# Issuing most of each x load from GpSimd as half rows in a pairwise bilinear kernel

## The chip, the cores and the metric

The kernel runs on one core of a Trainium2 chip. The metric is device time in microseconds (us), as the median of several executions; before the change it is 1336.65 us (1336.59 to 1337.08 over three). The profile is one execution with the hardware profiler, with a span of 1335.1 us.

## The reference

For 4096 samples with F = 32 features of D = 64 numbers each, every pair of features i < j (496 pairs) has its own 64 x 64 matrix. The output holds, for every sample and pair, the product of feature i with the pair's matrix, multiplied elementwise by feature j:

```python
i_idx, j_idx = np.triu_indices(F, k=1)
vi = inputs[:, i_idx, :]
vj = inputs[:, j_idx, :]
vdotw = jnp.einsum('bpd,pde->bpe', vi, W)
inter = vdotw * vj
return inter.reshape(B, -1)
```

All is float32. The input is 33.6 MB, the weights 8.1 MB, and the output 520 MB, so the output's bytes dominate.

## The kernel before

The samples are cut into NT = 32 tiles of 128, one sample per partition. Per tile, TensorE transposes x (in two halves), ScalarE (ACT) copies the transpose from PSUM to SBUF, TensorE multiplies it by the weights, VectorE multiplies the products in PSUM by x and writes them into a ring in SBUF, and SyncE (SP) issues four stores per tile from the ring.

x lives in a buffer of three slots, one tile each. Apart from the first and last tile, x is loaded two tiles at a time into neighbouring slots:

```python
STORES = [[0, 1], [2, 3], [4, 5, 6], [7, 8, 9, 10, 11, 12, 13, 14, 15]]
FIRST_HALF_AT, SECOND_HALF_AT = 9, 3
RING = 28160

def x_slots(NT):
    loads = [[(0, 0)]]
    for t in range(1, NT, 2):
        if t + 1 == NT:
            loads.append([(t, 1)])
        elif loads[-1][-1] == (t - 1, 2):
            loads.append([(t + 1, 0), (t, 1)])
        else:
            loads.append([(t, 1), (t + 1, 2)])
    return loads
```

This gives 17 loads: 2 of one tile and 15 of two. One load is one DMA from ACT's queue, in which each of the 128 partitions receives one contiguous row (8 KB for one tile, 16 KB for two):

```python
xbuf = const.tile([P, 3 * F * D], F32, tag="x", name="x")
...
def load_x(load):
    at = sum(len(before) for before in x_loads[: x_loads.index(load)]) * P * F * D
    n = len(load) * F * D
    s = load[0][1]
    nc.scalar.dma_start(
        out=xbuf[:, s * F * D : s * F * D + n],
        in_=x[at : at + P * n].rearrange("(p c) -> p c", p=P),
    )
```

The main loop starts the load of tile t + 1 at the start of tile t, and transposes the first half of x for tile t + 1 late in tile t (at row pair 9 of 16, within the last store's group):

```python
for t in range(NT):
    xt = slot[t]
    for load in x_loads:
        if min(load)[0] == t + 1:
            load_x(load)
    for s, group in enumerate(STORES):
        if at + store_w[s] > RING:
            at = 0
        osb = ring[:, at : at + store_w[s]]
        at += store_w[s]
        for p in group:
            if p == SECOND_HALF_AT:
                transpose_x(xt, 1)
            if p == FIRST_HALF_AT and t + 1 < NT:
                transpose_x(slot[t + 1], 0)
            ...  # matmuls into PSUM banks (line 170), VectorE multiplies into osb (lines 180, 188)
        nc.sync.dma_start(
            out=out[:, t * cols + o0 : t * cols + o0 + store_w[s]], in_=osb
        )
```

The four stores of a tile have rows of 30,208, 26,112, 31,488 and 39,168 bytes per partition, 126,976 bytes in all; the ring holds 112,640 bytes per partition. A part of the ring can be written again once the store that read it has landed.

Of the kernel before, what the change touches and what calls it, by code (L numbers as in the profile page):

```python
# [1 line left out]

# [6 lines left out]

F32 = mybir.dt.float32  # L10
ALU = mybir.AluOpType

P = 128
BANK = 512
BANKS = 8

STORES = [[0, 1], [2, 3], [4, 5, 6], [7, 8, 9, 10, 11, 12, 13, 14, 15]]

LOADS = [[0], [1], [2, 3], [4, 5, 6], [7, 8, 9, 10, 11, 12, 13, 14, 15]]
# [20 lines that stand above are left out]
@with_exitstack  # L40
def pair_bilinear_kernel(
    ctx: ExitStack,
    tc: tile.TileContext,
    x: bass.AP,
    w: bass.AP,
    out: bass.AP,
    F: int,
    D: int,
):

    nc = tc.nc
    NT = out.shape[1] * 2 // (F * (F - 1) * D)
    NPR = F // 2

    width = [(F - 1 - i) * D for i in range(F)]
    off = [sum(width[:i]) for i in range(F)]
    cols = sum(width)  # L80


    woff = [i % 2 * D + sum(width[i % 2 : i : 2]) for i in range(F)]
    store_w = [sum(width[2 * p] + width[2 * p + 1] for p in g) for g in STORES]

    const = ctx.enter_context(tc.tile_pool(name="const", bufs=1))
    psum = ctx.enter_context(tc.tile_pool(name="ps", bufs=1, space=bass.MemoryType.PSUM))

    ident = const.tile([P, P], F32, tag="ident", name="ident")
    make_identity(nc, ident)  # L90

    def runs(tl, a, b, n):

        ap = tl[:, a : a + n]
        return bass.AP(ap.tensor, ap.offset, [list(ap.ap[0]), [b - a, 2], list(ap.ap[1])])

    xbuf = const.tile([P, 3 * F * D], F32, tag="x", name="x")
    x_loads = x_slots(NT)
    slot = {t: xbuf[:, ts(s, F * D)] for load in x_loads for t, s in load}

    def load_x(load):

        at = sum(len(before) for before in x_loads[: x_loads.index(load)]) * P * F * D
        n = len(load) * F * D
        s = load[0][1]
        nc.scalar.dma_start(
            out=xbuf[:, s * F * D : s * F * D + n],
            in_=x[at : at + P * n].rearrange("(p c) -> p c", p=P),
        )

    pring = psum.tile([P, BANKS * BANK], F32, tag="pring", name="pring")
    bank = 0

    def take_banks(n):

        nonlocal bank
        if bank + n > BANKS:
            bank = 0
        got = pring[:, bank * BANK : (bank + n) * BANK]
        bank = (bank + n) % BANKS  # L120
        return got

    xT = const.tile([P, NPR * P], F32, tag="xT", name="xT")

    def transpose_x(xt, g):

        n = 2 * BANK // P
        pt = take_banks(2)
        for c in range(n):
            nc.tensor.transpose(pt[:, ts(c, P)], xt[:, ts(n * g + c, P)], ident)  # L130
        nc.scalar.copy(xT[:, ts(g, 2 * BANK)], pt)  # L131

    ring = const.tile([P, RING], F32, tag="ring", name="ring")
    at = 0

    load_x(x_loads[0])
    w_sb = const.tile([P, sum(width[0::2])], F32, tag="w", name="w")
    done = 0
    for g in LOADS:

        upto = woff[2 * g[-1]] + width[2 * g[-1]]
        nc.sync.dma_start(out=w_sb[:, done:upto], in_=w[:, done:upto])
        done = upto

    transpose_x(slot[0], 0)
# [10 lines that stand above are left out]
            o0 = off[2 * group[0]]  # L156
# [5 lines that stand above are left out]
                first = (width[2 * p] - 1) % BANK + 1  # L162
                for c1 in range(first, width[2 * p] + 1, BANK):
                    n = first if c1 == first else BANK
                    c0 = c1 - n
                    odd = width[2 * p + 1] and c1 > D
                    pm = take_banks(2)
                    for h in range(1 + bool(odd)):
                        a = woff[2 * p + h] + c0 - h * D
                        nc.tensor.matmul(  # L170
                            pm[:, h * BANK : h * BANK + n],
                            xT[h * D : (h + 1) * D, ts(p, P)],
                            w_sb[h * D : (h + 1) * D, a : a + n],
                            start=True,
                            stop=True,
                        )
                    xj = xt[:, (2 * p + 1) * D + c0 : (2 * p + 1) * D + c1]
                    o = [off[2 * p + h] - o0 + c0 - h * D for h in range(2)]
                    if odd and (c0 or c1 < width[2 * p]):
                        nc.vector.tensor_tensor(  # L180
                            runs(osb, o[0], o[1], n),
                            runs(pm, 0, BANK, n),
                            bass.AP(xj.tensor, xj.offset, [xj.ap[0], [0, 2], xj.ap[1]]),
                            ALU.mult,
                        )
                    else:
                        for h in range(1 + bool(odd)):
                            nc.vector.tensor_tensor(  # L188
                                osb[:, o[h] + h * D : o[h] + n],
                                pm[:, h * (BANK + D) : h * BANK + n],  # L190
                                xj[:, h * D :],
                                ALU.mult,
                            )
            nc.sync.dma_start(
                out=out[:, t * cols + o0 : t * cols + o0 + store_w[s]], in_=osb
            )


# [30 lines left out]
```

## Time and profile before

| what | value |
|---|---|
| median time | 1336.65 us |
| span of the profile | 1335.1 us |
| PE busy | 1160.6 us (87%) |
| VectorE (DVE) busy | 1183.4 us (89%) |
| ACT busy | 66.1 us (5%) |
| GpSimd (POOL) busy | 0.7 us |
| moved by DMA | 562.87 MB at 422 GB/s |
| VectorE waits for landed stores (line 180) | 102.6 us in 44 waits |
| from issue to landing, x loads of two tiles (median) | 20.4 us |

In the profile, a line of the page with forty digits gives the busy share in 40 equal slices of the span. "q1" is the DMA queue of SyncE and "q10" that of ACT. In the list of DMA issues the last number is the median time from issue to landing. In the chain of waits, each line has a start, a length, and what was waited for or worked on. In the timeline, the bracket at the end of a line says how long the engine was idle before it, and what ended that.

Besides these views the trace holds one record for each DMA packet, with its queue, start, duration and size. A packet here is one contiguous row, or a semaphore's write of 4 bytes at the end of a DMA on each of the 16 engines.

### The profile page before, as it was taken

What the parts mean: (1) busy time and instruction counts of PE and PEld (TensorE: products, weight loads), DVE (VectorE), ACT (ScalarE), POOL (GpSimd) and SP (SyncE); (2) the same over time, 40 slices, a digit from 0 to 9 for tenths busy, and PEclk for the clock granted to TensorE, in tenths of its full rate; (3) what the DMA queues carried; (4) which work ended last, traced back from release to release, by engine and by line L of the source; (5) the groups of instructions that cost most, each with busy time, mean ns of one, the idle gap of its engine ahead of it and who ended that gap; (6) DMA issues with size and microseconds to landing.
All of it is one profiled execution on the core that took longest, in us unless ns stands there. A gap on an engine that the chain in (4) does not pass through costs nothing.

```text
span 1335.1 us, 13080 instructions
## 1 busy us (share of the span) xinstructions
PE 1160.6 (87%) x5376; PEld 544.9 (41%) x5376; DVE 1183.4 (89%) x1376; ACT 66.1 (5%) x65; POOL 0.7 (0%) x6
## 2 busy tenths in 40 slices
PE   6998989989899898998989889798998979989893
PEld 3443334443344443444444444344443434354441
DVE  5998989989899898998989899898998989989894
ACT  0000000000000000000000000000000000000000
POOL 0000000000000000000000000000000000000000
PEclk9999999989899999998989999899999999989997
DMA  9999999999999999999999999999999999999998
GB/s 397 433 430 430 431 428 430 418 433 430 413 425 410 436 414 427 426 414 433 405 432 431 419 429 411 432 426 421 428 413 430 426 407 417 429 421 423 429 425 352
DMA packets 21659, 562.87 MB, mean 422 GB/s; under 512 B 2400, under 2 KB 2400, under 8 KB 2656
## 3 DMA queue, kind: packets, MB, share of 16 engines
q1 hardware_dynamic: 19152, 528.49, 92.8%
q10 hardware_dynamic: 2448, 33.56, 5.9%
q8 instruction: 42, 0.69, 0.2%
q14 instruction: 17, 0.14, 0.0%
HBM read 41.94 MB, written 520.09 MB: 421 GB/s over the span
## 4 chain that ended last, share of the span: by engine, by line
DMA 47%; DVE 38%; issue 9%; PE 5%; DVEq 0%; ACT 0%
DMA out_dram<-ring 46%; DVE ring L180 32%; DVE ring L188 5%; PE pring L170 5%; DMA x<-in_x_dram 1%; DVEq L180 0%; PE pring L130 0%; ACT xT L131 0%; DVEq L225 0%; DVEq L188 0%
## 5 line engine op out<-in xcount | busy, mean ns | idle before, releaser
L170 PE MATMUL pring<-w,xT 64*128 64x512 f32 (+4 forms) x4864 | 1098.4, 564 | 146.4 <-DVE ring L180 133.5
L180 DVE TENSOR_TENSOR ring<-pring,x 128x1024 f32<-128x1024 f32 (+3 forms) x1056 | 1104.1, 1108 | 131.4 <-DMA out_dram<-ring 102.6
L170 PEld LDWEIGHTS pring<-w,xT 64*128 64x128 f32 x4864 | 489.3, 191 | 711.7 <-DVE ring L180 533.0
L131 ACT COPY xT<-pring 128x1024 f32<-128x1024 f32 x64 | 64.8, 1012 | 1224.1 <-PE pring L130 1224.1
L188 DVE TENSOR_TENSOR ring<-pring,x 128x64 f32<-128x64 f32 (+3 forms) x320 | 97.7, 356 | 2.6 <-DMA out_dram<-ring 1.9
L130 PEld LDWEIGHTS pring<-ident,x 128*128 128x128 f32 x512 | 55.6, 142 | 58.8 <-DVE ring L180 50.2
L130 PE MATMUL pring<-ident,x 128*128 128x128 f32 x512 | 70.8, 282 | 8.6 <-DMA x<-in_x_dram 8.6
L131 ACT ACT_TABLE_LOAD x1 | 1.3, 1283 | 1.7 <-PEq L221 1.7
masks.py:199 POOL TENSOR_SCALAR_AFFINE_SELECT ident<-ident 128x128 f32<-128x128 f32 x1 | 0.3, 292 | 0.1
masks.py:197 POOL MEMSET ident<- 128x128 f32 x1 | 0.2, 204 | 0.3 <-POOLq L221 0.3
L221 POOL MEMSET const-bfloat16-1.0<- 128x1 bf16 x1 | 0.1, 101 | 0.0
L221 POOL MEMSET const-uint8-127<- 128x1 uint8 x1 | 0.1, 101 | 0.0
L221 POOL MEMSET const-float32-0.0<- 128x1 f32 x1 | 0.1, 98 | 0.2 <-issue 0.2
L221 POOL MEMSET const-float32-1.0<- 128x1 f32 x1 | 0.1, 98 | 0.0
## 6 DMA issues: line engine op xcount, KB each, us to landing
out_dram<-ring SPq DMA_DIRECT2D x32, 4896.0 KB, 17.7
out_dram<-ring SPq DMA_DIRECT2D x32, 3936.0 KB, 18.1
out_dram<-ring SPq DMA_DIRECT2D x32, 3776.0 KB, 18.3
out_dram<-ring SPq DMA_DIRECT2D x32, 3264.0 KB, 18.6
x<-in_x_dram ACTq DMA_DIRECT2D x15, 2048.0 KB, 20.4
w<-in_w_dram SPq DMA_DIRECT2D x1, 2592.0 KB, 28.1
x<-in_x_dram ACTq DMA_DIRECT2D x2, 1024.0 KB, 12.8
w<-in_w_dram SPq DMA_DIRECT2D x1, 2016.0 KB, 22.2
```

Source lines behind the costliest of these rows:

```text
L130: nc.tensor.transpose(pt[:, ts(c, P)], xt[:, ts(n * g + c, P)], ident)
L131: nc.scalar.copy(xT[:, ts(g, 2 * BANK)], pt)
L170: nc.tensor.matmul(pm[:, h * BANK : h * BANK + n], xT[h * D : (h + 1) * D, ts(p, P)], w_sb[h * D : (h + 1) * D, a : a + n], start=True, st ...
L180: nc.vector.tensor_tensor(runs(osb, o[0], o[1], n), runs(pm, 0, BANK, n), bass.AP(xj.tensor, xj.offset, [xj.ap[0], [0, 2], xj.ap[1]]), ALU ...
L188: nc.vector.tensor_tensor(osb[:, o[h] + h * D : o[h] + n], pm[:, h * (BANK + D) : h * BANK + n], xj[:, h * D :], ALU.mult,)
L221: nc = bacc.Bacc("TRN2", target_bir_lowering=False, num_devices=1)
```

## The change

The x load of two tiles is split by rows. Rows (partitions) 0 to 119 are issued from GpSimd, rows 120 to 127 from ACT. Each row comes as two halves of 8 KB that lie apart in DRAM, where the host has laid out all first halves of a load ahead of all second halves. The loads of one tile stay with ACT alone, and are halved as well. It is meant to take the bulk of the x loads off ACT's queue, and to let them go in smaller pieces beside the stores.

```diff
-        nc.scalar.dma_start(
-            out=xbuf[:, s * F * D : s * F * D + n],
-            in_=x[at : at + P * n].rearrange("(p c) -> p c", p=P),
-        )
+        slots = xbuf[:, s * F * D : s * F * D + n]
+        rows = x[at : at + P * n].rearrange("(h p c) -> p h c", h=2, p=P)
+        halves = slots.rearrange("p (h c) -> p h c", h=2)
+        k = P - P // 16 if len(load) == 2 else 0
+        if k:
+            nc.gpsimd.dma_start(out=halves[:k], in_=rows[:k])
+        nc.scalar.dma_start(out=halves[k:], in_=rows[k:])
...
-    x = np.concatenate([rows[:, [t for t, _ in load]].ravel() for load in x_slots(NT)])
+    x = []
+    for load in x_slots(NT):
+        of_load = rows[:, [t for t, _ in load]].reshape(P, 2, -1)
+        x.append(of_load.transpose(1, 0, 2).ravel())
+    x = np.concatenate(x)
```

## The prediction

> **What bounds the kernel now.** I read the page first, then the stretches by pair of tiles, then the chain of waits and VectorE's timeline over one pair (172 to 254 us), and last the packet records. From the page:
>
> ```profile
> DMA  9999999999999999999999999999999999999998
> ...
> q1 hardware_dynamic: 19152, 528.49, 92.8%
> q10 hardware_dynamic: 2448, 33.56, 5.9%
> ```
>
> The 16 DMA engines are full in every slice. The stores and w (q1) take 92.8% of their time, x (q10) 5.9%; instruction fetches take the rest. The stretches show the same for one pair of tiles (columns: busy time of PE, PEld, DVE, ACT, POOL, then the granted clock, DMA share, GB/s):
>
> ```profile
> 172.00:254.00 82.00, 72.44 (x340) 33.43 (x338) 74.13 (x89) 4.05 (x4) 0.00 (x0) 0.98 1.00 428
> 254.00:336.00 82.00, 72.28 (x340) 33.42 (x338) 74.18 (x87) 4.05 (x4) 0.00 (x0) 0.96 1.00 425
> 664.00:746.00 82.00, 73.11 (x340) 35.90 (x338) 74.15 (x88) 4.05 (x4) 0.00 (x0) 0.96 0.99 423
> ```
>
> A pair takes 82 us; VectorE has 74 us of work in it and TensorE's records 72, so neither is the first bound. The chain of waits shows how the DMA holds them:
>
> ```profile
> 169.89 2.33 DVE ring L188 x7
> 172.24 21.82 DMA out_dram<-ring
> ...
> 194.15 1.15 DVE ring L180 x2
> ...
> 214.00 1.42 DVE ring L188 x5
> 215.44 17.14 DMA out_dram<-ring
> ...
> 253.97 21.98 DMA out_dram<-ring
> ```
>
> This is a loop through the 110 KB ring. VectorE can't write the group of rows 4 to 6 until the big store (4896 KB, the last of the tile before) has landed; from there it takes 21.3 us (194.1 to 215.4) to the next big store. A big store takes 17.1 us alone, but 21.8 when the x load is issued beside it. The pair is 21.8 + 21.3 + 17.1 + 21.4 = 81.6 us by the loop, and the DMA's work is about as long. Two limits are nearly equal here. VectorE's waits in that stretch:
>
> ```profile
> 178.07 8.08 DVE L180 TENSOR_TENSOR ring<-pring,x 128x640 f32<-128x640 f32 x8 [1.47 <-DMA out_dram<-ring]
> 194.15 9.07 DVE L180 TENSOR_TENSOR ring<-pring,x 128x896 f32<-128x896 f32 x9 [4.42 <-DMA out_dram<-ring]
> 232.68 9.07 DVE L180 TENSOR_TENSOR ring<-pring,x 128x896 f32<-128x896 f32 x9 [1.30 <-DMA out_dram<-ring]
> ```
>
> 4.42 us in the tile with an x load, 1.30 us in the one without. The x load and its landing:
>
> ```profile
> x<-in_x_dram ACTq DMA_DIRECT2D x15, 2048.0 KB, 20.4
> ```
>
> It is issued at 172.25 and its last packet starts at 192.8; the transposes that read it come at 205.09, where they wait for VectorE's banks and not for x. So x has about 12 us to spare.
>
> **Room.** In the packet records an x row of 16 KB takes 611 ns, a half row of 8 KB (in the two one-tile loads) 309 ns, a big store's row of 39 KB 1448 ns, and rows of 26, 30 and 31 KB 968, 1119 and 1166 ns. I counted how many packets are open at each moment. Below 16 of them, there are some 165 engine-us between 25 and 1315 us, about 10 us per engine, nearly all in short holes ahead of the big store. Those ahead of a big store with x beside it are larger (6.9, 18.3, 9.0, 8.3, 11.0 engine-us at 336, 418, 500, 582 and 664) than the others (4.0, 4.4, 2.7, 5.1, 3.7). One more loss goes with x: the first big-store packet on each engine is stretched, by some 8 engine-us a load (0.5 us per engine, 7 us over 14 loads), and by about 0.3 engine-us where no x load begins. So at most 10 + 7 = 17 us can come back, 1.3%; the rest is bytes. A gain of over 2% (below 1310 us) is not in this.
>
> [...]x and big-store packets alternate on one engine (611, 1448, 611, 1448 ns), eight of each. [...]The trace here shows only the 128-row case (eight rows to an engine). [...]No transfer in this trace starts from GpSimd. [...]
>
> **The change part by part.**
> *Removed:* 15 ACT loads of 128 rows, 8 packets of 16 KB per engine each: 8 x 0.611 = 4.89 us per pair.
> *Added, bytes:* the same bytes as half rows. 2 x 309 - 611 = 7 ns more per row, 8 rows, 15 loads: 0.8 us per engine over the run.
> *Added, spread:* [...]A store has landed only when its slowest engine is done, so most of this stands on the path: I take +6.
> *Moved, turns:* beside the eight big-store packets now go eight half rows instead of eight whole ones: 8 x (0.611 - 0.309) = 2.4 us less ahead of the big store's landing, 21.8 -> 19.4. The loop shrinks to 79.2 us per pair, so the DMA's own work becomes the only limit and most of the holes should close: I take 7 of 10 us back.
> *Moved, the start of x:* store and x load were issued within 0.01 us (172.24 and 172.25)[...]. With x from GpSimd the store may start undisturbed; against that, ACT still issues 8 rows, and a fetch of instructions, a third queue, stretches its neighbours by a like amount (packets of 1166 ns become 1764 and 1535). I count half of the 7 us: -3.5.
> *The wait for x:* eight turns beside the big store, eight beside the next (8 x (1.448 + 0.309) + 8 x (1.119 + 0.309) = 25.5 us) instead of 16.5, so x lands 9 us later, at about 203[...]. The need is at 205. Just hidden, at zero cost in the centre.
> Sum: +0.8 + 6 - 7 - 3.5 = -3.7, so 1333; I take 1332[...].
>
> **Rivals.** *x becomes the wait.* [...]PE would stall up to 7 us in every pair, less the 4.42 us of waiting that VectorE has there, so 15 x 3 to 15 x 7, 1375 to 1440 us. The 12 us of spare time and the explicit halving of rows speak against it. *The uneven spread is the bound.* [...]+9 and no holes closed, 1340 to 1346. The nearly full engines speak for it; that instruction fetches already make single engines late by some 1.6 us in turn speaks for part of it being absorbed. *Nothing moves,* because bytes bound it: 1335 to 1338. The 99 to 100% share speaks for it; the larger holes beside x against it.
>
> **Range and chances.** The best case is an even spread with holes and stretching gone: 1336.65 - 15, 1321. The uneven case with a short stall for x reaches 1350. Eight in ten lie between. Over 2% faster needs more than the 17 us of room: 0.03. Over 2% slower (above 1363) needs the first rival: 0.10. Within 2%: 0.87.
>
> **What would show it.** The turns are right if the big store beside an x load lands in 19 to 20 us rather than 21.8 and VectorE's wait of 4.42 us falls below 3. The size is right if the new queue shows 8 KB packets of about 309 ns. The slack is right if no transpose waits for x. The spread is right if the 16 arrivals of a store come further apart beside x loads, half of them late by about 0.6 us. The start of x is right if the first big-store packets keep near 1448 ns. I am wrong if PE waits for x, if packets of 4 KB or less appear, or if the new queue's packets last much longer than their bytes.

## The result and the profile after

The changed kernel takes 1355.63 us (1355.16 to 1356.19) against 1336.84 us, a ratio of 1.0141 (95% interval 1.0127 to 1.0155). The change costs 18.8 us. That lies above the whole range of 1321 to 1350, and I had expected a small gain.

The page of the changed kernel, where q0 is GpSimd's new queue:

```profile
DMA  9999999999999999999999999999999999999998
...
q1 hardware_dynamic: 19152, 528.49, 92.1%
q0 software_dynamic: 4080, 29.49, 5.5%
q10 hardware_dynamic: 904, 4.06, 1.1%
```

The DMA engines are as full as before, with the same bytes, over a longer span (1353.4 us). So the DMA's time became less useful, which busy shares don't show. The bytes per time do, in two pairs of tiles (columns as in the prediction):

```profile
182.60:265.20 82.60, 73.30 (x338) 36.81 (x336) 73.95 (x87) 4.05 (x4) 0.74 (x1) 0.94 1.00 421
679.70:762.10 82.40, 72.42 (x338) 33.07 (x336) 73.89 (x87) 4.05 (x4) 0.74 (x1) 0.98 1.00 421
```

421 GB/s for 423 to 428, with VectorE's work unchanged at 74 us. VectorE's waits in one pair (its timeline):

```profile
188.79 8.08 DVE L183 TENSOR_TENSOR ring<-pring,x 128x640 f32<-128x640 f32 x8 [1.82 <-DMA out_dram<-ring]
203.67 9.07 DVE L183 TENSOR_TENSOR ring<-pring,x 128x896 f32<-128x896 f32 x9 [2.49 <-DMA out_dram<-ring]
214.55 7.44 DVE L183 TENSOR_TENSOR ring<-pring,x 128x1024 f32<-128x1024 f32 x7 [0.54 <-DMA out_dram<-ring]
243.96 9.08 DVE L183 TENSOR_TENSOR ring<-pring,x 128x896 f32<-128x896 f32 x9 [2.43 <-DMA out_dram<-ring]
```

The wait of 4.42 us did shrink, to 2.49, but the others grew (1.47 to 1.82, 1.30 to 2.43, and a new one of 0.54). The sum is the same: 7.2 us before, 7.3 now. And x:

```profile
x<-in_x_dram POOLq DMA_DIRECT2D x15, 1920.0 KB, 30.4
```

It lands 10 us later than before. Outside the start no transpose waits for it.

**Where the 18.8 us lie.** Two marks in the trace split them. The first regular x load (the first that waits for a free slot) is issued at 91.2 us before and at 100.2 after: 9.0 us are lost in the start. From there to the load 13 pairs of tiles later, one pair takes 81.92 us before and 82.56 after: 0.64 us, or 9.0 us over some 14 pairs. The start is visible in the chain of waits, first before, then after:

```profile
0.73 7.73 DMA x<-in_x_dram
8.46 0.14 issue
8.60 1.95 PE pring L130 x8
```

```profile
0.74 19.04 DMA x<-in_x_dram
19.78 0.14 issue
19.92 1.95 PE pring L133 x8
```

The first transposes come 11.3 us later, because the first tile's x lands at 19.8 us instead of 8.5. That x load isn't among those that the change gives to GpSimd. It is one tile, still on ACT, though in 4 KB pieces.

### The profile page after: what moved, and what is told of

Read it like the earlier page. It is cut to its first block, busy times and chain, and to the rows that moved or that the text cites. A ratio compares the mean times of both kernels' runs of the same rounds, so it can differ in the third digit from the quotient of the medians.

```text
span 1353.4 us, 13119 instructions
## 1 busy us (share of the span) xinstructions
PE 1164.1 (86%) x5376; PEld 545.0 (40%) x5376; DVE 1184.0 (87%) x1376; ACT 66.1 (5%) x65; POOL 11.9 (1%) x21
## 4 chain that ended last, share of the span: by engine, by line
DMA 52%; DVE 33%; issue 8%; PE 5%; DVEq 0%; ACT 0%
DMA out_dram<-ring 50%; DVE ring L183 29%; PE pring L173 5%; DVE ring L191 5%; DMA x<-in_x_dram 1%; PE pring L133 0%; DVEq L183 0%; ACT xT L134 0%; DVEq L232 0%; DVEq L191 0%
## 5 line engine op out<-in xcount | busy, mean ns | idle before, releaser
L133 PE MATMUL pring<-ident,x 128*128 128x128 f32 x512 | 71.4, 284 | 22.5 <-DMA x<-in_x_dram 19.9
L111 POOL DMA_DIRECT2D x<-in_x_dram x15 | 11.2, 744 | 1162.0 <-DVE ring L191 1161.6
```

Of the source, the lines that this page charges most:

```text
L111: nc.gpsimd.dma_start(out=halves[:k], in_=rows[:k])
```

## The experiments

All are compared with the kernel before in the same session (1336.7 to 1336.9 us). "Pair" is the mean over 13 pairs of tiles, "first load" the issue of the first regular x load, both from the trace; x(0) is the start of the first transposes. The same steady part can differ with the start ahead of it: all_gpsimd and start_as_before, which load alike after the start, differ by 0.14 us in the pair, and so do the changed kernel and second_load_act by 0.16. So differences of that size in the pair don't show a cause. An engine-us is a microsecond of one of the 16 DMA engines. The diffs are against the changed kernel.

| kernel | us | ratio (95%) | x(0) | first load | pair |
|---|---|---|---|---|---|
| before | 1336.84 | | 8.6 | 91.2 | 81.92 |
| changed | 1355.63 | 1.0141 (1.0127 to 1.0155) | 19.9 | 100.2 | 82.56 |
| second_load_act | 1345.42 | 1.0064 (1.0049 to 1.0079) | 11.9 | 92.5 | 82.40 |
| all_gpsimd | 1339.88 | 1.0023 (1.0013 to 1.0033) | 14.8 | 95.5 | 81.84 |
| split_112_16 | 1350.67 | 1.0103 (1.0088 to 1.0118) | 19.6 | 99.4 | 82.33 |
| halves_on_act | 1337.85 | 1.0008 (1.0000 to 1.0017) | 11.6 | 92.3 | 81.90 |
| act_120_8 | 1356.26 | 1.0146 (1.0131 to 1.0161) | 11.7 | 100.1 | 82.73 |
| act_112_16 | 1347.00 | 1.0075 (1.0059 to 1.0090) | 11.8 | 97.3 | 82.19 |
| columns | 1339.37 | 1.0018 (1.0011 to 1.0026) | 11.1 | 91.6 | 82.06 |
| gpsimd_120_8 | 1355.93 | 1.0145 (1.0130 to 1.0160) | 19.5 | 100.5 | 82.62 |
| act_two_columns | 1337.94 | 1.0009 (1.0000 to 1.0017) | 11.3 | | 81.9 |
| act_64_64 | 1348.82 | 1.0092 (1.0078 to 1.0105) | 11.7 | 97.6 | 82.24 |
| act_columns | 1340.74 | 1.0028 (1.0017 to 1.0039) | 11.3 | 90.4 | 82.21 |
| start_as_before | 1337.50 | 1.0005 (0.9997 to 1.0013) | 8.9 | 91.4 | 81.98 |

**The second load back on ACT's queue.**

```diff
-        k = P - P // 16 if len(load) == 2 else 0
+        k = P - P // 16 if len(load) == 2 and load is not x_loads[1] else 0
```

> Only the second load (tiles 1 and 2, issued at the very start) goes back to ACT's queue, where it stands behind the first tile's load; all else is as in the changed kernel. Theory Start: in the changed kernel the second load runs from its own queue beside the first tile's load, so the first transposes come 11.3 us later (19.9 for 8.6 us) and the first regular load is issued 9.3 us later (100.5 for 91.2 us). Then x of tile 0 lands near 9 to 10 us here and the time falls by about 9 us, to 1345 to 1348. Rival: it is the halving of the first tile's rows into 4 KB that delays it; then x of tile 0 still lands at 15 us or later and the time stays above 1351. Both: the steady part keeps its 82.56 us per pair of tiles.

1345.42 us, 10.2 us less, with the first load at 92.5 us. Theory Start holds. Its rival is part of it: x(0) comes at 11.9 us and not at 8.6, so the 4 KB pieces cost 3 us there, of which 1.1 us reach the first load (halves_on_act). The pair fell a little as well (82.40), which I had not expected, though its loads are those of the changed kernel.

**All rows from GpSimd.**

```diff
-        k = P - P // 16 if len(load) == 2 else 0
+        k = P if len(load) == 2 else 0
...
-        nc.scalar.dma_start(out=halves[k:], in_=rows[k:])
+        if k < P:
+            nc.scalar.dma_start(out=halves[k:], in_=rows[k:])
```

> All 128 rows of the two-tile loads from GpSimd as half rows, none from ACT. Theory Spread (the step I charged with 6 us): the extra row on eight engines makes the steady pair 82.56 us for 81.91; with 128 rows on 16 engines the pair falls to 81.9 or less, and with the start unchanged the time is 1344 to 1348. Theory Queues: a third queue and its own start cost the time, through the stretched packets beside each start; with ACT's part gone the time falls as well, to 1345 to 1350. Theory Software: the packets from GpSimd themselves come late and stretched (327 ns mean for 309); then nothing falls: 1352 to 1358.

1339.88 us and 81.84 us per pair. The time lies below all three forecasts. Theory Software falls: GpSimd's packets are one half row each, of 311 ns on average, and cost no more than ACT's of that size (314 ns on average before the change). Their load starts later (first packet a median 4.5 us after the issue, for ACT's 2.9 before the change), which is nearly hidden: outside the start, transposes wait 3.3 us for x, in six waits. The start gained too, which I had not expected: the first load comes at 95.5 and not at 100.2. Both Spread and Queues foresaw a fall, so this run doesn't part them.

**112 rows from GpSimd, 16 from ACT.**

```diff
-        k = P - P // 16 if len(load) == 2 else 0
+        k = P - P // 8 if len(load) == 2 else 0
```

> Rows 0 to 111 from GpSimd and the last 16 from ACT, still half rows: [...]with three queues as in the changed kernel. Theory Spread: the pair falls to 81.9 us or less, the time to 1344 to 1348. Theory Queues: the three queues and two starts per load remain, so the pair stays at 82.4 to 82.7 us and the time at 1352 to 1358. Read with the run in which GpSimd issues everything, it tells Spread from Queues.

1350.67 us, between the two forecasts; 82.33 us per pair is nearer to Queues. The cut that I had taken for even doesn't cure it; how GpSimd's 112 rows lie over the engines was not shown. This run is why I formed a third theory, Ports, for the next ones: the packets of a load cut by rows and those beside them stretch each other. Why they should was a guess.

**All from ACT, in halves.**

```diff
-        k = P - P // 16 if len(load) == 2 else 0
+        k = 0
```

> All rows of all loads from ACT, in half rows: only the finer pieces are left of the change. By my prediction's step of the turns, the big store beside an x load lands about 2.4 us sooner (19 to 20 us for 21.8), holes close, and the time is 1326 to 1332. Rival (bytes bound it, or the start of x sets the loss): 1334 to 1339. If half rows themselves cost, through twice the packets, it is 1340 or more. The first tile's load is in 4 KB pieces here too; if those lose to w's larger rows at the start, x of tile 0 lands later than 8.5 us by up to 3 us, and that is to be subtracted.

1337.85 us, 81.90 us per pair: the rival. VectorE's waits show what became of the finer turns:

```profile
177.82 8.08 DVE L183 TENSOR_TENSOR ring<-pring,x 128x640 f32<-128x640 f32 x8 [1.18 <-DMA out_dram<-ring]
192.43 9.07 DVE L183 TENSOR_TENSOR ring<-pring,x 128x896 f32<-128x896 f32 x9 [2.94 <-DMA out_dram<-ring]
203.44 7.43 DVE L183 TENSOR_TENSOR ring<-pring,x 128x1024 f32<-128x1024 f32 x7 [0.67 <-DMA out_dram<-ring]
232.85 9.07 DVE L183 TENSOR_TENSOR ring<-pring,x 128x896 f32<-128x896 f32 x9 [2.44 <-DMA out_dram<-ring]
```

From the packet records, the last packet of a big store with an x load beside it ends 19.3 us after its issue, for 21.5 before, so the step is right to 0.2 us. But the same x bytes now stand beside the stores that follow, and the big store without an x load ends after 17.8 us instead of 16.7. The wait of 4.42 us became 2.94 + 0.67, 1.30 became 2.44 and 1.47 became 1.18: 7.2 us in sum, as before. The holes did not close either. The holes below 16 open packets, counted from 25 us to 20 us before the end without gaps of under 10 ns, are 196 engine-us here and 167 before.

**The row split without GpSimd.**

```diff
-            nc.gpsimd.dma_start(out=halves[:k], in_=rows[:k])
+            nc.scalar.dma_start(out=halves[:k], in_=rows[:k])
```

> Rows 0 to 119 and rows 120 to 127 as two loads, both from ACT, half rows, nothing from GpSimd; to be compared with the run in which ACT issues all rows in one load (1337.85 us, 81.90 us per pair). Theory Spread: rows lie unevenly over the engines (9 rows on some, none on one), 0.6 us more per load on the fullest, so the pair is 82.3 to 82.5 us and the time 1343 to 1347. Theory Queues (two queues that start beside the store, one of them GpSimd's): with one queue nothing is lost, 81.9 us, 1337 to 1339. Theory Ports ([...]stretch each other's packets): slower as well, with store packets stretched.

1356.26 us, as slow as the change, with no GpSimd load at all. So it is the split by rows that costs, and GpSimd isn't needed for it. The pair (82.73) fits Spread in kind and exceeds its size; the start lost 8 us against halves_on_act too (100.1 for 92.3), although x(0) came no later. The spread shows in the packet records: ACT's queue has 377 semaphore packets, 2 x 16 for the one-tile loads and 15 x (15 + 8), for 16 in each of the 150 DMAs before the change (2400 packets under 512 B). I read that as 120 rows on 15 engines and 8 rows on 8. Linking each packet to the one that starts as it ends gives chains, which I take as one per engine: in the load issued at 430 us, 8 of them hold 18 half rows, 7 hold 15 to 17, and one none.

**The same with 112 and 16 rows.**

```diff
-        k = P - P // 16 if len(load) == 2 else 0
+        k = P - P // 8 if len(load) == 2 else 0
...
-            nc.gpsimd.dma_start(out=halves[:k], in_=rows[:k])
+            nc.scalar.dma_start(out=halves[:k], in_=rows[:k])
```

> Rows 0 to 111 and 112 to 127 as two loads, both from ACT, half rows[...]. Spread: even, so as the one load, 81.9 us per pair, 1337 to 1339. Queues: one queue, the same. Ports: [...]slower by 3 to 8 us, 1341 to 1346.

1347.00 us, 1 us above Ports' range. Each of the 30 loads has 16 semaphore packets, so all 16 engines take part, and still it is 9 us above halves_on_act: Spread alone falls. The start tells most. Landing of w's last piece, in the list of DMA issues, here and in halves_on_act:

```profile
w<-in_w_dram SPq DMA_DIRECT2D x1, 2592.0 KB, 35.0
```

```profile
w<-in_w_dram SPq DMA_DIRECT2D x1, 2592.0 KB, 28.3
```

w's load itself was not changed. The rows of 13 KB, in an earlier piece of w, take 635 ns on average here and 498 in the kernel before (846 in the changed kernel). Within this one trace, 31 of them end before the first packet of the 112-row load (11.06 us) and take 498 ns; the 32 that run beside it and end before 13.6 us take 714. The 16-row load is issued only at 13.79. In halves_on_act both stretches show 498. So a load of 112 rows alone slows the rows of w, before its second part is issued and without GpSimd's queue.

**Split by columns between GpSimd and ACT.**

```diff
...
+        if len(load) == 2 and load is not x_loads[1]:
+            k = n // 2 - n // 32
+            nc.gpsimd.dma_start(out=halves[:, :, :k], in_=rows[:, :, :k])
+            nc.scalar.dma_start(out=halves[:, :, k:], in_=rows[:, :, k:])
+        else:
+            nc.scalar.dma_start(out=halves, in_=rows)
```

> The load is split by columns instead of rows: GpSimd brings 7680 bytes of each half row of all 128 rows, ACT the other 512 bytes, so that each queue is even over 16 engines and ACT's share is one sixteenth as in the change. The second load is on ACT, as in that run (1345.42 us, 82.40 us per pair). Spread and Ports: even[...], so 81.8 to 82.0 us per pair, 1337 to 1340. Queues: still a second and third queue that start beside the store, so 82.3 us or more, 1344 to 1347.

1339.37 us, as Spread and Ports said for the time. Against second_load_act only the direction of the cut differs, and with it the number of engines on ACT's part (16 semaphore packets for 8 in each of 14 loads): 6 us. The pair of 82.06 us leaves at most 0.16 us, about 2 us in all, to the additional queue and the small pieces.

**120 and 8 rows, both from GpSimd.**

```diff
-        nc.scalar.dma_start(out=halves[k:], in_=rows[k:])
+            nc.gpsimd.dma_start(out=halves[k:], in_=rows[k:])
+        else:
+            nc.scalar.dma_start(out=halves, in_=rows)
```

> Rows 0 to 119 and rows 120 to 127 both from GpSimd as two loads, half rows, nothing from ACT but the one-tile loads; to be compared with the run in which GpSimd issues all rows in one load (1339.88 us, 81.84 us per pair). Spread: uneven, but [...]the extra is 0.0 to 0.3 us per pair, 1340 to 1344; [...]0.6 us, 1347. Queues: one queue fewer than in the change, so as the one load, 1339 to 1341. Ports: slower, 1345 to 1350, with stretched store packets as in the changed kernel.

1355.93 us, above every forecast (Ports' ended at 1350). It is a poor witness, though: here transposes wait for x, 67.8 us in 14 waits (19.5 of it at the start), which no theory had foreseen. Spread's two figures rested on how GpSimd's rows lie over the engines, which no trace shows.

**Two controls on ACT, and a split by 64 rows.** First, all rows twice, by halves of the columns:

```diff
...
+        if len(load) == 2:
+            nc.scalar.dma_start(out=halves[:, 0], in_=rows[:, 0])
+            nc.scalar.dma_start(out=halves[:, 1], in_=rows[:, 1])
+        else:
+            nc.scalar.dma_start(out=halves, in_=rows)
```

> Control: each two-tile load as two loads from ACT, the first halves of all 128 rows, then the second halves; even, [...]one queue, two loads as in the split by 112 and 16 rows (1347.00 us). If it is the number of loads that costs, 1344 us or more. If it is where the rows lie (Ports or Spread), as the one load of halves: 1336 to 1340 us, 81.8 to 82.0 us per pair, w's rows of 13 KB at the start near 500 ns.

1337.94 us. The number of loads costs nothing here; but each half is one tile and was issued as its slot came free, about 41 us apart, so the pair isn't quite comparable. Second, the same cut by rows:

```diff
...
+        if len(load) == 2:
+            nc.scalar.dma_start(out=halves[: P // 2], in_=rows[: P // 2])
+            nc.scalar.dma_start(out=halves[P // 2 :], in_=rows[P // 2 :])
+        else:
+            nc.scalar.dma_start(out=halves, in_=rows)
```

> Each two-tile load as two loads from ACT of 64 rows each, half rows: 4 + 4 rows on each engine, so even in bytes, one queue[...]. Spread: even, so as the control, 1336 to 1340 us. Ports: worse than 112 and 16 rows (1347.00 us), 1347 to 1365 us, with w's rows at the start and the store packets beside x loads stretched, and x's own packets well over 309 ns while alone with each other.

1348.82 us. The chains show 16 half rows on each engine, and yet w's last piece lands late and the pair is 82.24 us:

```profile
w<-in_w_dram SPq DMA_DIRECT2D x1, 2592.0 KB, 35.8
```

w's 13 KB rows take 704 ns. The store packets hold 18.1 engine-us more per pair than at their fastest (the tenth percentile of each size), for 13.2 in halves_on_act. The time lies in Ports' forecast. Third, a control that issues both parts together:

```diff
-        k = P - P // 16 if len(load) == 2 else 0
+        k = n // 2 - n // 16 if len(load) == 2 else 0
...
-            nc.gpsimd.dma_start(out=halves[:k], in_=rows[:k])
-        nc.scalar.dma_start(out=halves[k:], in_=rows[k:])
+            nc.scalar.dma_start(out=halves[:, :, :k], in_=rows[:, :, :k])
+        nc.scalar.dma_start(out=halves[:, :, k:], in_=rows[:, :, k:])
```

> A closer control for the split by 112 and 16 rows (1347.00 us): every two-tile load as two loads from ACT in one eighth and seven eighths, but cut by columns (7168 and 1024 bytes of each half row, all 128 rows), issued together. Ports: [...]1337.5 to 1341 us (256 packets more per load cost at most 16 x 8 ns per engine and load, 2 us over 15), 81.9 to 82.1 us per pair, w's last piece landed 28 us after its issue. If two loads issued together cost what the split by rows cost: 1345 us or more and w at 34 us or more.

```profile
x<-in_x_dram ACTq DMA_DIRECT2D x15, 1792.0 KB, 28.0
x<-in_x_dram ACTq DMA_DIRECT2D x15, 256.0 KB, 44.0
w<-in_w_dram SPq DMA_DIRECT2D x1, 2592.0 KB, 28.2
```

1340.74 us, with the start undisturbed (w at 28.2, the first load at 90.4). At the start, the second load's second part is issued at 1.7 us here and at 13.7 to 13.8 in the cuts by rows, but the rows of w stretch there before that, as act_112_16 shows. That settles the start: two loads cut by columns leave w alone, two cut by rows delay it by 7 us. For the pair it is no clean control: 82.21 us are as long as with the cut by rows. But the time goes elsewhere: x's packets hold 102 engine-us per pair for 79.4 in halves_on_act, since the pieces of 1 KB take 46 ns and those of 7 KB 347; the store packets hold only 3.4 more than at their fastest, for 18.4 in act_112_16.

**Start as before, all rows from GpSimd after it.**

```diff
...
+        if load in x_loads[:2]:
+            nc.scalar.dma_start(out=slots, in_=x[at : at + P * n].rearrange("(p c) -> p c", p=P))
+        elif len(load) == 2:
+            nc.gpsimd.dma_start(out=halves, in_=rows)
+        else:
+            nc.scalar.dma_start(out=halves, in_=rows)
```

(with the first two loads left unhalved on the host)

> The first two loads as before the change (whole rows, ACT), the other two-tile loads as half rows of all 128 rows from GpSimd. What was measured apart: the start as before (91.2 us to the first regular load), 81.84 us per pair for 81.92. Sum: 1336.8 - 14 x 0.08 = 1335.7, so 1334.5 to 1337. If GpSimd's loads do close the holes once the start is out of the way, as I had predicted, 1328 to 1333. If the 81.84 was chance, 1336 to 1338.

1337.50 us, 1.0005 (0.9997 to 1.0013), 81.98 us per pair: there is no gain, and each of its executions is a little above each of the kernel before. Undoing the start and the row split accounts for the loss of 18.8 us but for 0.7.

## Why the prediction was wrong

The sum was -3.7 us and the change cost +18.8. Of the 22.5 us between, 9.0 are the start, which the sum lacked; 7 and 3.5 are gains that didn't come; 2.2 are what the steady part lost beyond the +6 and +0.8 of the sum. The last 0.8 lies outside the two marks in the trace.

- **What bounds it, and the room:** right. Every version keeps the DMA engines full, and none beat the kernel before.
- **The start:** missing, and half the loss (9.0 of 18 us). I worked out 15 loads as if all were regular, and didn't see that the second load is issued at time zero beside the first. On ACT's queue it stood behind the first tile's x; on a queue of its own it runs among its packets. Before, the second load's first packet starts at 7.63 us and the first tile's last packet ends at 7.93. In the changed kernel, GpSimd's first packet starts at 5.67 us and the first tile's last ends at 17.68; in between 162 of GpSimd's packets start, and the first tile's packets last 244 ns on average, for 170 until then. x(0) goes 8.6 -> 11.6 us by the 4 KB pieces (halves_on_act), -> 14.8 by the second queue (all_gpsimd), -> 19.9 by the split of rows (changed); the first regular load goes 91.2 -> 92.3 -> 95.5 -> 100.2 us.
- **Spread, +6:** the direction was right, the reason incomplete. How a load of fewer than 128 rows lies over the engines, on which the 6 us rested, was not shown by the trace that I had. That a store lands with its slowest engine is in that trace: of the big store issued at 172.24 us the first of 16 semaphore packets starts at 190.11 us and the last at 193.56, and VectorE, which waits for it, goes on only at 194.1. The pair lost 0.64 us, 9.0 us in all. On ACT the cut 112/16, with all 16 engines in each load, costs 0.29 us per pair (act_112_16 less halves_on_act) and 5 us at the start; 120/8 costs 0.83 per pair and 8 at the start. So the uneven spread adds 0.54 us per pair, near the 0.62 us of two half rows more (2 x 309 ns; eight of the chains hold 18 for 16), and the rest came with the cut 112/16. From GpSimd it is less (pairs of 82.40 to 82.56 us, for 82.73); why was not shown.
- **Why a cut by rows costs:** the runs show that packets stretch, and not why; the guess behind the name Ports is not shown. At the start the rows of w stretch (498 -> 635 ns in act_112_16, 704 in act_64_64, 846 in the changed kernel), also where each engine holds 16 half rows (act_64_64). In the steady part the store packets hold 18.4 engine-us per pair more than at their fastest in act_112_16 and 18.1 in act_64_64, for 13.2 in halves_on_act. But not every packet of such a cut is stretched: in split_112_16, 12 of the half rows of ACT's 16 rows that start within 0.15 us (at 346.9 us) take 309 to 318 ns. In the steady part the link is weaker than at the start, since the closest control was disturbed.
- **Turns, -7:** failed at the step from a shorter landing to closed holes. The landing went 21.5 -> 19.3 us as worked out, but the big store without x beside it went 16.7 -> 17.8, the waits moved to other stores, and the holes stayed (196 engine-us for 167). The pair kept its length (halves_on_act: 81.90 us for 81.92).
- **Start of each x load, -3.5:** failed, though its sign came true. The first 16 packets of a big store beside x are 0.7 engine-us over 1448 ns each in all_gpsimd (1.9 in the changed kernel), for 7.7 before. But the other 112 packets are now 9.5 over it (7.6 in the changed kernel), for 0.9 before. The stretch moved to later packets, so there was nothing to gain.
- **Packet overhead, +0.8:** the packets show it (the two-tile loads hold 0.9 us more per engine in halves_on_act), but the time doesn't: of the 1.0 us that halves_on_act costs, 1.1 lie at the start and none in the pair.
- **The wait for x, 0:** as expected. In the changed kernel x's landing 10 us later was hidden.
- **The rivals:** in the changed kernel x did not become the wait outside the start, and GpSimd's 3600 packets of x were 8 KB; what the stall of up to 7 us rested on was not shown. The uneven spread as the bound, 1340 to 1346, fits the steady part in number (1345.4 with the start mended). That is partly luck, since cuts by rows with all 16 engines in each load lose time as well (1347.00 us in act_112_16, 1348.82 in act_64_64).

## What to carry to other kernels

Where the DMA engines were full, a new order of the same bytes gained nothing in any of these versions, and a cut by rows lost 9 to 19 us. If a load has to be cut, try columns first and keep all 128 rows in each part; that cost 1 to 4 us here. A load moved to another queue loses its place behind earlier loads (x(0) 11.6 -> 14.8 us); look at what is issued at time zero, and keep the first needed transfer first in its queue. When one wait in a full loop shrinks, add up all waits of the loop before you count a gain.

## What the runs showed of the hardware that I had not expected

- Unchanged packets of w last 1.3 to 1.7 times as long (498 to 635 and 846 ns for 13 KB) while x rows of a 112- or 120-row load are moved (498 and 714 ns within one trace, act_112_16), but not beside a 128-row load from a queue of its own (503 ns in all_gpsimd).
- GpSimd's packets were whole half rows of 8 KB, with a median of 309 ns in the changed kernel; beside running stores the first comes a median 4.5 us after the issue (all rows) and 5.0 us (120 rows), for 2.9 us from ACT.
- Fetches of instructions, 42 packets of 16 KB and about 1 us, fall on changing engines (the first six on six different chains); each delays its engine by an estimated 1.3 to 1.9 us, with the 0.4 to 1.0 us by which the packets beside it are stretched (before the change, between 126 and 313 us).
